# One term less in the softmax denominators of the second four heads, and one chunk's residual added by identity products

## The chip, the core and the metric

The kernel runs on one core of a Trainium2 chip. The metric is the device time of one execution in microseconds. Three runs of the kernel before gave 3167.57, 3167.66 and 3168.4 us; the median is 3167.66 us. All times below are of the kernel before.

## What is computed

The reference is one attention layer with a mask from an adjacency matrix, a feed forward part and three layer norms. There are F = 8 graphs of N = 2048 nodes with C = 256 channels, in H = 8 heads of D = 32 channels. Cut to what matters:

```
q, k, v = split(x @ w_qkv)                        # per head: N x 32
scores  = where(adj > 0, q k^T / sqrt(32), -1e9)
attn    = softmax(scores)                         # over the keys m
t       = attn @ v
y       = layernorm1(x + t)
z       = layernorm2(y + relu(y @ w1 + b1) @ w2 + b2)
out     = layernorm(x + z)                        # the last residual and norm
```

All of it is in 32-bit floats. The mask is added to the scores instead of being selected, and the softmax is not divided until the end: the exponentials are multiplied with v, their sums over the keys (the denominators) are found beside that, and the result is divided by them.

## The kernel before, in words

**Steps.** The main loop runs over `items` = (f, qc, g, mb): graph, chunk of 512 queries (4 of them), group of four heads (g = 0 or 1) and block of 128 keys (mb = 0 to 15). That makes 1024 steps of one block each; 16 steps are a group, 32 steps a chunk, 128 steps a graph. Step t issues, in this order: one piece of side work (`advance`), the exponentials of block t + 1 (L283, ScalarE), the scores of block t + 2 (L276, TensorE) with the mask added to them out of PSUM by VectorE (L279), and the products of block t with v (L310, TensorE). So TensorE's queue holds side work, scores, values, side work, and so on. A block is a tile `p` of 128 keys x 4 heads x 512 queries, 1 MB in 32-bit floats; 12 buffers hold such tiles.

**PSUM.** Six of the eight banks hold scores (three pairs; a block takes two pairs), one bank holds the sum of the value products, and one is left for side work. So at most one piece of side work can start in a step.

**Side work.** Generators in the list `fill` yield when they want to wait some steps, when they need the bank (BANK), when they could go on with the bank that they hold (MORE), or when they hold it and must wait (WAIT). The list is sorted by due time. `advance` gives each step a credit of 2200 units. One set of products (four of 128x512, one for each 32 columns of the array) costs 2048, four transposes cost 1400, so a step takes one such piece. A piece that is past its due time, or that stands in the way of one that is, goes on without credit, and then a step holds two sets. Side work is: turning x, projecting it to q, k and v for the next groups and the next graph, the denominators, the division (`outcome`, `divide`), and the `tail` of a chunk (norm, feed forward, norm, last residual, norm).

**Denominators.** The 16 blocks of a group are first added up to four tiles outside TensorE (`add_up`): the chain `POOLED` by GpSimd's `tensor_tensor` (L339), the two chains `MOVED` by accumulating DMAs that GpSimd issues (L336), and block 15 (`ALONE`) stays as it is. Then `denominator` multiplies the four tiles with `halves` (ones in 16 of 32 columns), one set of products a tile (L382), all into one PSUM bank. For g = 0 the sum is copied to `dT` (L385). For g = 1 it is added to `dT` by VectorE (L388), turned by TensorE (L95), and its reciprocal `rc` taken (L395); then `outcome` is started, which turns the two halves of the output, multiplies them with `rc` (L427) and adds the first residual by an accumulating DMA (L414).

The generator is started at step t + 2 after a group's last block t, with due time t + 8; the pooled tile is not used before step t + 3 and the second moved tile not before t + 4. The order on all queues is the order of issue, so a product whose tile is late holds up the scores and values behind it.

**The residual of the last graph's third chunk.** For (f, qc) = (7, 2) the first residual is no DMA: x is loaded early into the tile `xb` (L745, L746), and `outcome` has VectorE add it to y (L411, 128x1024, both operands in SBUF) before it starts the tail (which uses `xb` once more for its last residual). The very last group, `ENDING` = (7, 3, 1), has code of its own (`closing`) and is untouched.

Of the kernel before, what the change touches and what calls it, by code (L numbers as in the profile page):

```python
# [16 lines left out]
ALU = mybir.AluOpType  # L17
# [12 lines left out]
BANK, MORE, WAIT, TURNED, ROOM, INPUTS = -1, -2, -3, -4, -5, -10  # L30
# [31 lines left out]
def fast_path(ctx, tc, cst, x, adj, out, RS):  # L62
    nc = tc.nc
    F, N, C = x.shape
    NCK, TPC, MB = N // CH, CH // P, N // P
# [19 lines left out]
    ident, identb, wqkv, w1s, w2s = cst["ident"], cst["identb"], cst["wqkv"], cst["w1s"], cst["w2s"]  # L85
    state = {"pair": 0, "side": None, "turn": 0, "turned": False, "holder": None, "tails": 0, "credit": 0}

    def columns(out, lhsT, rhs, start, stop):
        state["credit"] -= 4 * out.shape[-1]
        in_columns(nc, out, lhsT, rhs, start, stop)  # L90
# [11 lines left out]
    def bank(dt=F32):  # L102
        shape = [P, CH] if dt == F32 else [P, 2, CH]
        if state["side"] is not None:
            i = 1 - state["side"]
            return ps_x[i].tile(shape, dt, name=f"x{i}")
        i = state["turn"]
        state["turn"] = (i + 1) % 5
        pool = ps_s[i] if i < 3 else ps_x[i - 3]
        return pool.tile(shape, dt, name=f"s{i}" if i < 3 else f"x{i - 3}")  # L110
# [140 lines left out]
    PT, O, OT, RC, DT = {}, {}, {}, {}, {}  # L251
# [63 lines left out]

    POOLED = (0, 3, 6, 8, 10, 12, 14)
    MOVED = ((1, 4, 7, 11), (2, 5, 9, 13))
    ALONE = 15  # L320

    SUM = 4

    def add_up(item):
        f, qc, g, mb = item
        if item[:3] == ENDING:
            h = mb // (MB // 2) * (MB // 2)
            if mb - h in (2, 4):
                first = PT[f, qc, g, h]
                nc.gpsimd.tensor_tensor(first, first, PT.pop(item), ALU.add)  # L330
            elif mb - h == 3:
                nc.gpsimd.dma_start(PT[f, qc, g, h + 1], PT.pop(item), accum_op=ALU.add)
            return
        for chain in MOVED:
            if mb in chain[1:]:
                nc.gpsimd.dma_start(PT[f, qc, g, chain[0]], PT.pop(item), accum_op=ALU.add)  # L336
        if mb in POOLED[1:]:
            first = PT[f, qc, g, POOLED[0]]
            nc.gpsimd.tensor_tensor(first, first, PT.pop(item), ALU.add)  # L339


# [24 lines left out]

    def denominator(f, qc, g, ready):
        grp = (f, qc, g)
        blocks = [ALONE, MOVED[0][0], POOLED[0], MOVED[1][0]]
        late = {2: ready - 1, 3: ready}  # L370
        yield BANK
        ps = bank()
        for n, block in enumerate(blocks):
            if n:
                yield MORE
            while state["now"] < late.get(n, 0):
                yield WAIT
            term = PT.pop((f, qc, g, block))
            state["credit"] -= 4 * CH
            for h in range(4):  # L380
                r = D * h
                nc.tensor.matmul(ps[r:r + D, :], cst["halves"][:, g, :], term[:, h, :], start=(n == 0), stop=(n == len(blocks) - 1))  # L382
        if g == 0:
            DT[f, qc] = op.tile([P, CH], F32, name="dT")
            nc.scalar.copy(DT[f, qc], ps)  # L385
            return
        dT = DT.pop((f, qc))
        nc.vector.tensor_tensor(dT, ps, dT, ALU.add)  # L388
        yield 1
        yield BANK  # L390
        ps = bank()
        transposes(ps, [dT[:, j::TPC] for j in range(TPC)])
        rc = RC[f, qc] = op.tile([P, TPC, H], F32, name="rc")
        den = ps.rearrange("p (j c) -> p j c", c=P)[:, :, ::D // 2]
        nc.vector.reciprocal(rc, den)  # L395
        nc.vector.tensor_tensor(RS[:, 0], RS[:, 0], den, ALU.add)
        nc.vector.tensor_tensor(RS[:, 1], RS[:, 1], den, ALU.min)
        begin = items.index((f, qc, g, LAST)) + SUM + 2
        start(begin, outcome(f, qc), begin)

    def outcome(f, qc):
        yield ROOM
        state["tails"] += 1
        xin = x[f, qc * CH:(qc + 1) * CH, :].rearrange("(p j) c -> p j c", p=P)
        y = yp.tile([P, TPC, C], F32, name="y")
        begin = items.index((f, qc, 1, LAST)) + SUM + 2
        yield from divide(f, qc, y)
        if (f, qc) == (F - 1, NCK - 2):
            yield 1
            xb = state["xb"]  # L410
            nc.vector.tensor_tensor(y, y, xb, ALU.add)  # L411
            start(begin + 3, tail(f, qc, y, xin, 2, xb), begin + 18)
            return
        nc.gpsimd.dma_start(y, xin, accum_op=ALU.add)  # L414
        if (f, qc) == (F - 1, NCK - 3):
            start(begin + 10, tail(f, qc, y, xin, 2), begin + 18)
        else:
            start(begin + 10, tail(f, qc, y, xin), begin + 26)
# [12 lines left out]
    def tail(f, qc, y, xin, per=1, xb=None):  # L431
        yield from norm(y, per)
        yield from feed_forward(y)
        if xb is not None:
            nc.gpsimd.tensor_tensor(xb, xb, rows(cst["be2r"]), ALU.add)
        yield 1
        z = y
        yield from norm(z, per if per == 1 else TPC)
        while xb is None and per > 1 and state["now"] % MB not in CALM:
            yield 1  # L440
        nc.gpsimd.tensor_tensor(z, z, rows(cst["g2r"]), ALU.mult)  # L441
        yield 1
        nc.gpsimd.tensor_tensor(z, z, rows(cst["be2r"]) if xb is None else xb, ALU.add)  # L443
        yield 1
        if xb is None:
            nc.gpsimd.dma_start(z, xin, accum_op=ALU.add)
            yield 7 if per == 1 else 10
        yield from norm(z, per)
        nc.sync.dma_start(out[f, qc * CH:(qc + 1) * CH, :].rearrange("(p j) c -> p j c", p=P), z)
        state["tails"] -= 1  # L450
# [155 lines left out]
    def start(t, gen, due):  # L606
        fill.append([t, gen, 1, due])
        fill.sort(key=lambda e: e[3])
# [120 lines left out]
    for t, (f, qc, g, mb) in enumerate(items):  # L729
        if g == 1 and mb % 2 and (f + 1 < F or qc + 1 < NCK):  # L730
            t0 = t
            while ((qc + 1) % NCK, mb // 2) not in MADE:
                advance(t0, finish=True)
                t0 += 1
            load_mask(f + (qc + 1) // NCK, (qc + 1) % NCK, mb // 2)
        while n_mask < MB and t >= 2 + 3 * n_mask:
            start(t, mask_job(n_mask), 3 * MB - 2 + 2 * n_mask if n_mask < MB // 2 else 4 * MB - 2 + 2 * n_mask)
            n_mask += 1
        for what, *which in (NEXT if f else {**NEXT, **LATER}).get(t % FRAME, []):
            to = f if what is ask and which[0] else f + 1  # L740
            if to < F:
                at = (0, 0, 0) if what is turn else (which[0], 0, 0) if what is ask else (0, which[1], which[0] * TPC)
                start(t, what(to, *which), t + 3 * MB if what is turn else items.index((to, *at)) - LEAD - 1)
        if t == len(items) - 2 * MB - 6:
            state["xb"] = take([P, TPC, C], F32)  # L745
            nc.sync.dma_start(state["xb"], x[f, qc * CH:(qc + 1) * CH, :].rearrange("(p j) c -> p j c", p=P))  # L746
        if t == len(items) - MB:
            xr, xb = state["rows"] = [take([P, TPC, C], F32) for _ in range(2)]
            nc.sync.dma_start(xr.rearrange("p (h j) c -> p h j c", h=2),
                              x[f, qc * CH:(qc + 1) * CH, :].rearrange("(h p j) c -> p h j c", h=2, p=P))  # L750
        if t == len(items) - MB + 6:
            nc.gpsimd.tensor_tensor(xb, xr, rows(cst["be2r"]), ALU.add)
        if t:
            advance(t)

        if t + 1 < len(items):
            exponentials(items[t + 1])
        if t + LEAD < len(items):
            nf, _, ng, nmb = items[t + LEAD]
            t0 = t  # L760
            while (nf, nmb // TPC, ng) not in V:
                advance(t0, finish=True)
                t0 += 1
            scores(items[t + LEAD])
        values(items[t])
        add_up(items[t])
        if mb == LAST and t + 1 < len(items):
            start(t + 2, denominator(f, qc, g, t + SUM), t + SUM + 4)
        for h in range(2):
            if t == len(items) - MB // 2 * (2 - h) + 4:  # L770
                start(t + 1, closing(h), len(items) - h)
    t = len(items)
# [244 lines left out]
```

## Time and profile before, and how to read it

| what | value |
|---|---|
| median of the runs | 3167.66 us |
| the profiled execution's own time | 3165.28 us |
| its span (first to last instruction) | 3163.5 us |
| granted TensorE clock | 0.995 of full speed |
| VectorE: mask added to the scores, L279, x2016 | 2371.1 us busy, 1218 ns each |
| ScalarE: exponentials, L283, x1024 | 1955.8 us busy, 1910 ns each |
| TensorE: scores L276 and values L310, x8064 each | 1152.4 and 1075.3 us busy |
| accumulating DMAs of tiles `p`, x380 | 1024.0 KB each, 10.1 us from issue to landing |

A row of the groups gives line, engine, operation, output <- inputs, count, then the busy time in us, the mean of one in ns, and the idle time of the engine ahead of it with what ended it. The profile shows a 32-bit product as two records, so a set of four products is 8 records; the four run side by side in the array. In the timeline the columns are start and duration in us, engine, line, operation, tiles, shape and count, and in brackets the idle time of the engine just before with what released it. The windows view gives busy time of PE (TensorE), PEld (weight loads), DVE (VectorE), ACT (ScalarE) and POOL (GpSimd) in a stretch of time.

### The profile page before, as it was taken

To read this page: it belongs to the slowest core of one execution; us is meant where nothing else is said; L and a number is where in the kernel's file an instruction comes from. 1 tells how busy PE (TensorE), PEld (TensorE's weight loads), DVE (VectorE), ACT (ScalarE), POOL (GpSimd) and SP (SyncE) were. 2 spreads that over 40 slices of the span, in tenths; PEclk is the share of its full clock that TensorE was granted. 3 is DMA by queue.
4 is the path that set the end of the run, shared out by engine and by line. 5 is a ranking of instruction groups with operands and counts; after the bars stand their busy time and mean duration, and the time that the engine had idled before them with its cause. 6 is when DMAs were issued, how large, how long until landed. Compare 5 with 4: busy or idle time off the path is not lost.

```text
span 3163.5 us, 68998 instructions
## 1 busy us (share of the span) xinstructions
PE 3071.6 (97%) x29220; PEld 969.5 (31%) x29220; DVE 2751.4 (87%) x3138; ACT 2423.8 (77%) x1934; POOL 2589.8 (82%) x1358
## 2 busy tenths in 40 slices
PE   8899999999999999999999999999999999999986
PEld 4222233222332233322333323323233323332223
DVE  4989888998888998888988898888888888889885
ACT  4777777777778877778877878777778777778774
POOL 1768888888888988888888888888889888889885
PEclk9999999999999999999999999999999999999998
DMA  8998888988888988789878888879879888888861
GB/s 255 224 213 187 189 184 182 205 189 192 178 176 202 198 186 182 167 197 218 186 168 187 191 199 192 180 174 204 193 172 205 178 192 193 177 174 167 174 149 42
DMA packets 165467, 586.89 MB, mean 186 GB/s; under 512 B 15360, under 2 KB 84480, under 8 KB 116512
## 3 DMA queue, kind: packets, MB, share of 16 engines
q0 software_dynamic: 63696, 430.60, 69.0%
q1 hardware_dynamic: 100640, 150.50, 14.1%
q8 instruction: 231, 3.78, 0.5%
q10 hardware_dynamic: 816, 1.31, 0.1%
q14 instruction: 84, 0.69, 0.1%
HBM read 146.15 MB, written 37.75 MB: 58 GB/s over the span
## 4 chain that ended last, share of the span: by engine, by line


## 5 line engine op out<-in xcount | busy, mean ns | idle before, releaser
L279 DVE TENSOR_TENSOR p<-s,mask 128x1024 f32<-128x1024 f32 x2016 | 2371.1, 1218 | 302.3 <-PE s L276 170.2
L283 ACT ACTIVATE p<-p 128x2048 f32<-128x2048 f32 x1024 | 1955.8, 1910 | 565.3 <-DVE p L279 458.2
L339 POOL TENSOR_TENSOR p<-p 128x2048 f32<-128x2048 f32 x378 | 1845.1, 4881 | 332.7 <-ACT p L283 332.2
L276 PE MATMUL s<-qT,kT 32*128 32x512 f32 x8064 | 1152.4, 640 | 48.1 <-DVE p L279 44.7
L310 PE MATMUL x<-p,v 128*32 128x512 f32 x8064 | 1075.3, 605 | 3.0 <-ACT oT L314 3.0
L276 PEld LDWEIGHTS s<-qT,kT 32*128 32x128 f32 x8064 | 315.5, 183 | 653.6 <-DVE p L279 627.7
L336 POOL DMA_DIRECT2D p<-p x378 | 406.5, 1076 | 69.7 <-ACT p L283 49.4
L310 PEld LDWEIGHTS x<-p,v 128*32 128x32 f32 x8064 | 158.7, 108 | 768.2 <-issue 303.5
L382 PE MATMUL x<-p,halves 128*32 128x512 f32 x2016 | 261.1, 592 | 0.3 <-ACT turned L575 0.3
L54 PE MATMUL x<-in,wqkv 128*32 128x512 f32 x1888 | 245.6, 592 | 1.5 <-DVE y L170 0.8
L360 ACT ACTIVATE y<-y,nb,rs 128x256 f32<-128x256 f32 x372 | 218.3, 591 | 1.5 <-POOL nb L357 1.4
L348 DVE BATCH_NORM_STATS2 st<-y 128x6 f32<-128x256 f32 x372 | 154.7, 416 | 0.0
L54 PE MATMUL x<-turned,w1s 128*32 128x512 f32 (+1 forms) x1024 | 127.1, 593 | 0.0
L54 PEld LDWEIGHTS x<-wqkv,in 128*32 128x32 f32 x3584 | 102.2, 110 | 62.9 <-issue 54.5
L54 PE MATMUL x<-w2s,hT 128*32 128x256 f32 x2016 | 120.3, 379 | 0.0
L54 PE MATMUL x<-wqkv,in 128*32 128x128 f32 x3584 | 117.1, 273 | 0.0
L382 PEld LDWEIGHTS x<-p,halves 128*32 128x32 f32 x2016 | 65.4, 110 | 149.8 <-issue 147.2
L54 PEld LDWEIGHTS x<-in,wqkv 128*32 128x32 f32 x1888 | 61.1, 110 | 143.4 <-issue 115.1
L354 POOL TENSOR_TENSOR rs<-rs,mhalf 128x4 f32<-128x4 f32 x93 | 96.2, 1035 | 7.7
L441 POOL TENSOR_TENSOR y<-y,g2r 128x1024 f32<-128x1024 f32 x31 | 100.4, 3240 | 0.0
L443 POOL TENSOR_TENSOR y<-y,be2r 128x1024 f32<-128x1024 f32 x30 | 92.1, 3071 | 0.6
L54 PEld LDWEIGHTS x<-w2s,hT 128*32 128x32 f32 x2016 | 65.4, 110 | 68.9 <-issue 35.3
(155 smaller groups left out, 1423.1 us busy)
## 6 DMA issues: line engine op xcount, KB each, us to landing
p<-p POOLq DMA_DIRECT2D x380, 1024.0 KB, 10.1
in<-xd SPq DMA_DIRECT2D x87, 512.0 KB, 8.7
mask<-md SPq DMA_DIRECT2D x248, 128.0 KB, 8.5
y<-in_x_dram POOLq DMA_DIRECT2D x60, 512.0 KB, 9.7
out_dram<-y SPq DMA_DIRECT2D x31, 512.0 KB, 5.9
in<-in_x_dram SPq DMA_DIRECT2D x30, 512.0 KB, 10.3
xd<-in SPq DMA_DIRECT2D x28, 512.0 KB, 8.3
p<-in_adj_dram SPq DMA_DIRECT2D x8, 1024.0 KB, 14.1
```

Source lines behind the costliest of these rows:

```text
L54: nc.tensor.matmul(out[r:r + D], lhsT[:, r:r + D], rhs, start=start, stop=stop)
L276: nc.tensor.matmul(ps2[half][:, j, :], KT[f, mb // TPC, g][r:r + D, (mb % TPC) * P:(mb % TPC + 1) * P], QT[f, qc, g][r:r + D, :], start=Tr ...
L279: nc.vector.tensor_tensor(pt[:, 2 * half:2 * half + 2, :], ps, MK[f, qc, mb // 2][:, mb % 2, None, :].to_broadcast([P, 2, CH]), ALU.add)
L283: nc.scalar.activation(PT[item], PT[item], AF.Exp, scale=1.0 / math.sqrt(D))
L310: nc.tensor.matmul(O[grp][r:r + D, :], V[f, mb // TPC, g][:, mb % TPC, r:r + D], PT[item][:, h, :], start=(mb == 0), stop=(mb == LAST))
L336: nc.gpsimd.dma_start(PT[f, qc, g, chain[0]], PT.pop(item), accum_op=ALU.add)
L339: nc.gpsimd.tensor_tensor(first, first, PT.pop(item), ALU.add)
L348: nc.vector.bn_stats(st, t[:, j, :])
L354: nc.gpsimd.tensor_tensor(rs, rs, cst["mhalf"], ALU.pow)
L360: nc.scalar.activation(t[:, j, :], t[:, j, :], AF.Identity, bias=nb[:, j:j + 1], scale=rs[:, j:j + 1])
L382: nc.tensor.matmul(ps[r:r + D, :], cst["halves"][:, g, :], term[:, h, :], start=(n == 0), stop=(n == len(blocks) - 1))
L441: nc.gpsimd.tensor_tensor(z, z, rows(cst["g2r"]), ALU.mult)
```

## The change

For g = 1 block 15 is no longer left alone: it becomes the last member of GpSimd's chain, which gets eight members instead of seven, and the moved chains shift by one block. `denominator` then has three tiles instead of four, is started two steps later, with late times and due time two steps later too. The group g = 0 stays as it is. Apart from this, in the third chunk of the last graph, the residual x is added to y not by VectorE from SBUF but with two sets of products of the identity with `xb`, whose results VectorE adds to y out of PSUM in two halves; the tail starts at the earliest one step later.

```diff
-    POOLED = (0, 3, 6, 8, 10, 12, 14)
-    MOVED = ((1, 4, 7, 11), (2, 5, 9, 13))
+    POOLED = ((0, 3, 6, 8, 10, 12, 14), (0, 3, 5, 7, 9, 11, 13, 15))
+    MOVED = (((1, 4, 7, 11), (2, 5, 9, 13)), ((1, 4, 8, 12), (2, 6, 10, 14)))
     ALONE = 15
...
-        for chain in MOVED:
+        for chain in MOVED[g]:
...
-        if mb in POOLED[1:]:
-            first = PT[f, qc, g, POOLED[0]]
+        if mb in POOLED[g][1:]:
+            first = PT[f, qc, g, POOLED[g][0]]
             nc.gpsimd.tensor_tensor(first, first, PT.pop(item), ALU.add)
...
     def denominator(f, qc, g, ready):
         grp = (f, qc, g)
-        blocks = [ALONE, MOVED[0][0], POOLED[0], MOVED[1][0]]
-        late = {2: ready - 1, 3: ready}
+        one, two = (chain[0] for chain in MOVED[g])
+        blocks = [one, POOLED[g][0], two] if g else [ALONE, one, POOLED[g][0], two]
+        late = {1 + (g == 0): ready - 1, 2 + (g == 0): ready}
...
         yield from divide(f, qc, y)
         if (f, qc) == (F - 1, NCK - 2):
-            yield 1
             xb = state["xb"]
-            nc.vector.tensor_tensor(y, y, xb, ALU.add)
-            start(begin + 3, tail(f, qc, y, xin, 2, xb), begin + 18)
+            for j in range(0, TPC, 2):
+                yield BANK
+                ps = bank()
+                columns(ps, ident, xb[:, j:j + 2, :].rearrange("p j c -> p (j c)"), start=True, stop=True)
+                nc.vector.tensor_tensor(y[:, j:j + 2, :], ps.rearrange("p (j c) -> p j c", c=C), y[:, j:j + 2, :], ALU.add)
+            start(begin + 4, tail(f, qc, y, xin, 2, xb), begin + 18)
             return
...
         if mb == LAST and t + 1 < len(items):
-            start(t + 2, denominator(f, qc, g, t + SUM), t + SUM + 4)
+            start(t + 2 + 2 * g, denominator(f, qc, g, t + SUM + 2 * g), t + SUM + 4 + 2 * g)
```

## The prediction

> **What bounds the kernel now.** The first part of the page comes first:
>
> ```profile
> PE 3071.6 (97%) x29220; PEld 969.5 (31%) x29220; DVE 2751.4 (87%) x3138; ACT 2423.8 (77%) x1934; POOL 2589.8 (82%) x1358
> ```
>
> TensorE (PE) looks like the bound, but VectorE and GpSimd are near it, and both get or lose work here. Next the groups that the change touches:
>
> ```profile
> L339 POOL TENSOR_TENSOR p<-p 128x2048 f32<-128x2048 f32 x378 | 1845.1, 4881 | 332.7 <-ACT p L283 332.2
> L336 POOL DMA_DIRECT2D p<-p x378 | 406.5, 1076 | 69.7 <-ACT p L283 49.4
> L382 PE MATMUL x<-p,halves 128*32 128x512 f32 x2016 | 261.1, 592 | 0.3 <-ACT turned L575 0.3
> ```
>
> L382 is 2016 records, 8 a set: 252 sets, 1.04 us busy each. PE waited 0.3 us ahead of them in all, so no sum of p came late. Then the timeline, cut at the first score product (L276) of each step. A step with one set of side work, and one without:
>
> ```profile
> 1728.49 1.14 PE L276 MATMUL s<-qT,kT 32*128 32x512 f32 x8
> 1729.56 1.06 PE L310 MATMUL x<-p,v 128*32 128x512 f32 x8
> 1730.44 1.04 PE L54 MATMUL x<-in,wqkv 128*32 128x512 f32 x8
> 1731.42 1.14 PE L276 MATMUL s<-qT,kT 32*128 32x512 f32 x8
> 1732.49 1.06 PE L310 MATMUL x<-p,v 128*32 128x512 f32 x8
> 1733.97 1.14 PE L276 MATMUL s<-qT,kT 32*128 32x512 f32 x8 [0.42 <-DVE p L279]
> ```
>
> From one L276 to the next is 2.93 us with a set, 2.55 without: the empty step is bound by VectorE, which masks two score tiles (2 x 1.218). So **an emptied slot is worth 2.93 - 2.55 = 0.38, not a set's 0.975** (2.925/3). A step made to take two sets is longer:
>
> ```profile
> 1659.70 1.14 PE L276 MATMUL s<-qT,kT 32*128 32x512 f32 x8
> 1661.66 1.93 PE L54 MATMUL x<-wqkv,in 128*32 128x128 f32 x64
> 1663.52 1.14 PE L276 MATMUL s<-qT,kT 32*128 32x512 f32 x8
> ```
>
> It takes 3.82, so **a double turned into two singles is worth 0.89**. VectorE's cover is read in the windows view, over the steps that hold a chunk's denominators and division:
>
> ```profile
> 1785.23:1808.34 23.11, 22.77 (x181) 6.90 (x177) 22.34 (x31) 15.48 (x9) 14.65 (x12) 1.00 0.63 138
> 1704.44:1708.22 3.78, 3.78 (x36) 0.99 (x32) 3.58 (x5) 1.96 (x2) 3.78 (x1) 1.00 1.03 210
> ```
>
> VectorE (third figure after the length) has 0.77 us free in the first 23.11 us, 0.59 of it in the first step, and 0.20 in the second stretch. What is taken from PE there is had only up to that.
>
> **What the Trainium skill says.** "GPSIMD Engine Reference", 3.1, has 4497 ns for a tensor_tensor add of 2048 32-bit elements; here adds in line start 4.5 us apart when nothing lies between. "SBUF — State Buffer", Who interferes with whom: a VectorE instruction with two SBUF inputs is fully blocked while a GpSimd instruction reads SBUF. The trace agrees:
>
> ```profile
> 3044.71 4.52 POOL L339 TENSOR_TENSOR p<-p 128x2048 f32<-128x2048 f32 x1 [0.28 <-ACT p L283]
> 3045.31 5.01 DVE L411 TENSOR_TENSOR y<-y,in 128x1024 f32<-128x1024 f32 x1
> 3051.51 2.09 PE L276 MATMUL s<-qT,kT 32*128 32x512 f32 x8 [5.06 <-DVE p L279]
> ```
>
> L411 ends 1.09 us after the add. "VectorE: DVE Perf Modes", The TRN2 errata, prices a 32-bit tensor_tensor at (N + 151)/0.96 ns: 1.22 us for 1024, so some 3.8 of the 5.01 is waiting.
>
> **The change, part by part.** There are 32 groups with g = 1; all but the last lose a set: 31. Write +k for k steps after a group's block 15.
>
> (1) Where the slot goes. In graphs 1 to 7 the four chunk ends differ.
> - After chunk 4 (7 times, at step 514 in the middle of the trace) the sets sit at +3 to +6. Now +3 is free. A projection to v waits there (its k was copied out at 1575, before; it ran at +10, +11), so it takes +3 and +4, the denominators +5 to +7, all that follows comes one slot earlier, and the double of 1659.70 becomes two singles. VectorE has 0.28 us free in that step and 1.26 in the next, so I count nearly all: 7 x 0.86 = 6.0.
> - After chunk 1 (7 times) w2 products fill the slots to +5; three sets follow at +6, +7 and, due, a double at +8 (1704.44). It becomes a single: 3.78 - 2.92 = 0.86, but VectorE has 0.20 there and 0.17 in the next step: 7 x 0.4 = 2.8 (bounds 0.2 and 0.86).
> - After chunk 2 (8 times) a turn of x whose load landed at 1775.4 can take +3; side work moves up and one more empty step comes, where VectorE may be full: 8 x 0.35 = 2.8 (0 to 0.4).
> - After chunk 3 (8 times, 1878.57) the next projection's loads landed at 1878.0 and 1880.8 and it waits five steps from issue, so +3 stays empty: 8 x 0.37 = 3.0. That slot ends before VectorE's full stretch, which then begins earlier.
> - The first graph's first chunk: 0.3. Sum **14.9 us**.
>
> (2) GpSimd. An add more for each of 31 groups: 31 x 4.881 = 151 us busy, 82% to 87%. It is hidden as long as the tiles are ready at +4, +5, +6. I laid out the tightest kind (chunk 3, before step +3 at 1878.57) with the trace's own ends of the exponentials and spacings: add 4.5, issue 0.65 to 0.8, g1 and be1 2.3 each, a norm's four small ones 2.2. The old chain idles around blocks 5 to 8 (2.2 and 1.3 us) and ends at 1880.8; the new one starts at block 5, has no such gap, and ends at 1881.7, against a use at 1886.0 (the old 1886.37 less 0.37). The first moved tile's last DMA is issued at 1870.4; with landings of 9 to 11 us it is there at 1879 to 1882, used at 1883.1. The second: issued 1875.6, there at 1885 to 1887, used at 1889.0. So 2 to 4 us stay. After chunk 2 the same comes out (1 to 3 us for the first tile); after 4 there is a step more, after 1 some 15 us. The longest landing in the trace is 14.3 us, so I take a wait of 0.1 us in each of the 16 tight groups, **1.5 us lost**. Bounds: nothing, and 2.5 us each. Moved DMAs stay six a group; their issue on GpSimd shifts by a block. SP's queue and its loads only follow the side work. Norms queue behind adds on GpSimd and ScalarE waits for them in order, with the exponentials behind; around 1859 the norm follows an add and ScalarE starts 0.06 us after it. In the new order it follows a DMA issue and is 1.4 us earlier; after chunk 2 it is 0.7 later, with 1.2 to spare. I take nothing (bounds -0.5 and +1 each). The 12 buffers: block 15 is released by an add ending near +4 instead of a product at +3, as many as before; nothing.
>
> (3) The residual. Gone: the stall of 5.06 us. Added: two sets in steps that were empty (2 x 0.38), two evictions of 128x512 like L427's 0.68 us beside them. The denominators there start two steps later but nothing else waits, and two more steps are empty. Steps from 3021.3 to 3068.0 took 46.7 us; laid out anew by kind (3 sets 2.93, 3 turns 2.74, 2 identity sets 2.93, 2 empty 2.58, 4 with norm statistics about 3.46) they take 41.9. The tail starts two steps later, so its last norm runs deeper in the end: -4.8 + 0.8 = **4.0 us saved** (bounds 1 and 6).
>
> Sum: 14.9 - 1.5 + 4.0 = 17.4 us. The profiled execution goes from 3165.28 to 3147.9 (span 3146.1); the median lies 2.38 above it, so 3167.66 - 17.4 = **3150.3 us**, its own range 3143 to 3156.
>
> **Rivals.**
> - Full price: PE is all that counts, each set is worth 0.975: 31 x 0.975 - 2 x 0.975 + 5.06 = 33: 3134. For: 97% busy. Against: the empty step at 1731.42.
> - Covered: empty slots give nothing as VectorE is full after them; only the doubles after chunk 4 and the residual count, 6 + 4 = 10: 3158. For: 0.77 us in 23 us. Against: 0.59 of it is in the very step that is emptied.
> - Late sums, some: a wait of 1 us in 16 groups eats 16: 3167, no change.
> - **Slower**: the first moved tile (last block 12, not 11) lands after +4, and scores behind it starve a VectorE that has no slack. The place is chunks 2 and 3; from 1.5 us a group (24 us) it decides against the 17.4 + 1.5. At 2.5 us: 40 - 18.9 = 21: 3189. For: GpSimd runs without a gap from block 5, landings up to 14.3. Against: the layout above.
>
> **Chances.** Forecast 0.60, full price 0.10, covered 0.15, some late 0.09, slower 0.06. Within 0.2% (6.3 us) is about what a measurement of this kernel can't tell from no change. Faster 0.85, same 0.09, slower 0.06. The range 3138 to 3167 takes in the covered and some-late cases and leaves out most of full price and slower, under 2 in 10.
>
> **What would show it.** L382 at 1768 records; L339 x409; empty steps of 2.55 at +3 after chunk 3; no 64-record step near block 9 of g = 1 after chunk 4; GpSimd near 2740 us; no 5 us L411. Wrong if L382 waits for POOL or a DMA by over 0.5 us a group, or if steps behind an empty one show PE waiting for DVE by as much as was saved.

## The result, and the profile after

The changed kernel takes 3158.14 us in the median of 8 runs (3156.47 to 3159.73), the kernel before 3167.91 us in 8 runs on the same chip. The ratio is 0.9969, with a 95% interval of 0.9960 to 0.9978: **9.8 us faster**, a little over half of the 17.4 us of the forecast. The time lies inside the wide range of the prediction (3138 to 3167), but above the range that its forecast gave itself (3143 to 3156). The profiled execution took 3158.02 us, its span 3155.97 us.

The first part of the page and the groups of the pooled sum and of the denominators, after:

```profile
PE 3051.3 (97%) x28988; PEld 962.6 (31%) x28988; DVE 2747.6 (87%) x3139; ACT 2427.1 (77%) x1934; POOL 2727.7 (86%) x1389
...
L339 POOL TENSOR_TENSOR p<-p 128x2048 f32<-128x2048 f32 x409 | 1999.9, 4890 | 221.3 <-ACT p L283 200.4
L383 PE MATMUL x<-p,halves 128*32 128x512 f32 x1768 | 231.1, 594 | 1.6 <-DVE kT L170 1.4
```

The denominators' sets (L383 now) have lost 248 records, 31 sets; GpSimd has 31 adds and 138 us more; and PE waited 1.6 us ahead of the sets in all, 1.4 of it for a tile of the mask jobs. So the sums are not late. VectorE's time is the same within 4 us. But PE waits for VectorE ahead of its scores more than before, 108 times in place of 90. These are the lines of PE's waits, first before, then after (us in all, times, the longest):

```profile
PE s L276 <- DVE p L279: 44.7, 90, 5.1
```

```profile
PE s L276 <- DVE p L279: 52.6, 108, 2.3
```

In the before figure is the one stall of 5.1 us at the old residual. Without it PE's waits for VectorE went from 40 to 53 us. That is a first sign of where a part of the missing gain went.

Cut at the first score product of a block, the two traces stand so (us; blocks are counted over the whole loop, so block 128 begins graph 1):

| stretch | before | after | difference |
|---|---|---|---|
| start and graph 0 | 436.34 | 439.27 | +2.9 |
| graph 1 to graph 7, chunk 3 | 2579.14 | 2569.59 | -9.6 |
| of these, one of graphs 2 to 6, mean | 381.37 | 379.94 | -1.4 |
| graph 7, chunk 4, up to the scores of block 1007 | 49.19 | 44.20 | -5.0 |
| the end, from there on | 98.84 | 102.91 | +4.1 |

The first row needs care. Over all twelve traces of this study graph 0 ends between 436.2 and 442.3 us, and the start alone lies between 53.2 and 57.5, with an order that is the same there. The profiled run of the kernel before was among the earliest. From the end of graph 0 on the traces repeat: graphs 2 to 6 take 379.93 to 379.95 us each after. The steady graphs give 7.2 of the 9.6 us and graph 7's first three chunks 2.8; graph 1 takes 0.4 us longer than before (382.58 against 382.19), and why it gains nothing was not worked out.

The forecast has 7.6 us more than the measured gain. Of these, 2.7 lie in the second row (12.3 forecast, 9.6 found) and 3.4 in the last two rows together (4.0 for the residual and 0.3 for the denominators forecast, 0.9 found). What is left, about 1.5, falls to the start and graph 0 when the medians are taken.

### The profile page after: what moved, and what is told of

It is laid out like the page before. It is cut to its first block, busy times and chain, and to the rows that moved or that the text cites. A ratio compares the mean times of both kernels' runs of the same rounds, so it can differ in the third digit from the quotient of the medians.

```text
span 3156.0 us, 68508 instructions
## 1 busy us (share of the span) xinstructions
PE 3051.3 (97%) x28988; PEld 962.6 (31%) x28988; DVE 2747.6 (87%) x3139; ACT 2427.1 (77%) x1934; POOL 2727.7 (86%) x1389
## 4 chain that ended last, share of the span: by engine, by line
## 5 line engine op out<-in xcount | busy, mean ns | idle before, releaser
L339 POOL TENSOR_TENSOR p<-p 128x2048 f32<-128x2048 f32 x409 | 1999.9, 4890 | 221.3 <-ACT p L283 200.4
L336 POOL DMA_DIRECT2D p<-p x378 | 416.2, 1104 | 49.2 <-ACT p L283 41.0
L383 PE MATMUL x<-p,halves 128*32 128x512 f32 x1768 | 231.1, 594 | 1.6 <-DVE kT L170 1.4
L360 ACT ACTIVATE y<-y,nb,rs 128x256 f32<-128x256 f32 x372 | 218.3, 591 | 0.5 <-POOL nb L357 0.5
L348 DVE BATCH_NORM_STATS2 st<-y 128x6 f32<-128x256 f32 x372 | 154.8, 416 | 0.0
L383 PEld LDWEIGHTS x<-p,halves 128*32 128x32 f32 x1768 | 57.3, 110 | 133.9 <-issue 126.5
```

The source lines that it names most:

```text
L348: nc.vector.bn_stats(st, t[:, j, :])
L360: nc.scalar.activation(t[:, j, :], t[:, j, :], AF.Identity, bias=nb[:, j:j + 1], scale=rs[:, j:j + 1])
```

## Experiments

| kernel | median, us | ratio to before, 95% |
|---|---|---|
| den_only | 3161.37 | 0.9977 (0.9966 to 0.9987) |
| res_only | 3167.76 | 0.9996 (0.9988 to 1.0004) |
| no_fifteen | 3158.31 | 0.9965 (0.9952 to 0.9979) |
| early | 3172.70 | 1.0013 (1.0007 to 1.0020) |
| first_old | 3157.79 | 0.9964 (0.9950 to 0.9978) |
| two_old | 3159.18 | 0.9967 (0.9955 to 0.9979) |
| gap | 3149.13 | 0.9934 (0.9921 to 0.9948) |
| three_stats | 3149.26 | 0.9934 (0.9920 to 0.9948) |
| before_gap | 3170.98 | 1.0005 (0.9998 to 1.0012) |
| gap_two_old | 3145.63 | 0.9926 (0.9913 to 0.9940) |

The kernel before had 3168.60, 3168.63 and 3168.87 us in the three comparisons.

**The two parts alone.** `den_only` is the changed kernel with the old residual; `res_only` is the kernel before with the new one.

```diff
-            for j in range(0, TPC, 2):
-                yield BANK
...
+            yield 1
+            nc.vector.tensor_tensor(y, y, xb, ALU.add)
+            start(begin + 3, tail(f, qc, y, xin, 2, xb), begin + 18)
```

> The changed kernel with the old residual of the last graph's third chunk (one VectorE add after the division); only the denominators and the sums are new. The forecast's own terms (1) and (2), 14.9 - 1.5 = 13.4 us saved, would give 3154.5. Theory from the two traces (a steady graph gains only 1.3 us, graph 0 loses 4.7 in one stall, graph 7's first three chunks gain 2.8, the start 1.1): 8 to 9 us saved, 3159 to 3160. If the 4.1 us that the end grew by come from the denominators (two more empty steps, sums ending later) and not from the residual, less than 6 saved, 3162 or more.

> The kernel before with only the residual as identity products. Forecast's term (3): 4.0 us saved, 3163.9. Theory: the stall of 5 us goes, but the tail of that chunk then runs about 4 us deeper into the end, so 0.5 to 1.5 us saved, 3166.4 to 3167.4; the end after step 1007 is longer than before by 3 to 4 us here too. Rival: the longer end belongs to the denominators; then the end is as before and 4 to 5 us are saved, 3163 to 3164.

The denominators alone save 7.2 us (3168.6 to 3161.4). That falls between the theory (8 to 9 us) and its rival (less than 6), so neither number came out. The residual alone saves 0.8 us, as its theory said; it can't be told from nothing. By the traces, graph 7's chunk 4 becomes 2.1 us shorter in den_only, 4.4 in res_only and 5.0 with both, and the end 2.0, 2.9 and 4.1 us longer. So the longer end belongs to both parts, more to the residual. What the residual's 4.4 us consist of is seen in the timelines, first of den_only, then of the changed kernel:

```profile
3040.45 4.85 POOL L339 TENSOR_TENSOR p<-p 128x2048 f32<-128x2048 f32 x1
3042.38 4.01 DVE L412 TENSOR_TENSOR y<-y,in 128x1024 f32<-128x1024 f32 x1
3047.58 1.48 PE L276 MATMUL s<-qT,kT 32*128 32x512 f32 x8 [4.05 <-DVE p L279]
```

```profile
3038.60 4.89 POOL L339 TENSOR_TENSOR p<-p 128x2048 f32<-128x2048 f32 x1
3038.71 1.04 PE L54 MATMUL x<-in,ident 128*32 128x512 f32 x8
3040.53 0.68 DVE L415 TENSOR_TENSOR y<-x,y 128x512 f32<-128x512 f32 x1
3041.64 1.04 PE L54 MATMUL x<-in,ident 128*32 128x512 f32 x8
```

The VectorE add with two inputs in SBUF takes 4.01 us and ends 1.1 us after the GpSimd add beside it; an add of half the size with one input in PSUM, under a GpSimd add of the same length, takes 0.68 us. In "SBUF — State Buffer", Who interferes with whom, the Trainium skill says that a VectorE instruction with at most one SBUF input, outside the modes that use two ports, does not contend with GpSimd; the 0.68 us agree.

Why the end is longer is seen around the last copy of the output oT, first before, then after. L490 (L494 after) are the denominators' products of the last group's closing halves, L467 (L471 after) the norms of the two halves, L360 the last norm of chunk 3's tail.

```profile
3123.46 1.91 PE L490 MATMUL x<-p,halves 128*32 128x256 f32 x32
3123.71 0.37 ACT L303 COPY oT<-x 128x256 f32<-128x256 f32 x1 [2.38 <-PE x L298]
3134.09 1.09 ACT L467 ACTIVATE y<-y,nb,rs 128x256 f32<-128x256 f32 x2 [10.01 <-DVE nb L465]
...
3150.56 2.31 ACT L467 ACTIVATE y<-y,nb,rs 128x256 f32<-128x256 f32 x4 [3.25 <-DVE nb L465]
...
3158.23 1.09 ACT L467 ACTIVATE y<-y,nb,rs 128x256 f32<-128x256 f32 x2 [0.19 <-DVE nb L465]
```

```profile
3113.18 4.50 PE L494 MATMUL s<-p,halves 128*32 128x256 f32 x80
3113.43 0.37 ACT L303 COPY oT<-x 128x256 f32<-128x256 f32 x1 [1.19 <-PE x L298]
3125.50 1.09 ACT L471 ACTIVATE y<-y,nb,rs 128x256 f32<-128x256 f32 x2 [11.69 <-DVE nb L469]
...
3142.36 1.09 ACT L471 ACTIVATE y<-y,nb,rs 128x256 f32<-128x256 f32 x2 [5.21 <-DVE nb L469]
3143.35 1.08 ACT L360 ACTIVATE y<-y,nb,rs 128x256 f32<-128x256 f32 x2
...
3150.03 1.09 ACT L471 ACTIVATE y<-y,nb,rs 128x256 f32<-128x256 f32 x2 [0.19 <-DVE nb L469]
```

The tail's last norm (L360) now stands between the norms of the halves, and one might blame it. But from 3150.56 to 3158.23 before, and from 3142.36 to 3150.03 after, it is 7.67 us both times, so that costs nothing. The time is lost ahead of it. The later tail holds up the closing halves' sums, which start right behind its last w2 products: 18.9 us ahead of the last copy of oT before, 15.4 after. So 80 records of them (4.50 us) are left at the copy, against 32 (1.91 us), and the first norm of the halves starts 12.1 us after the copy, against 10.4. That is 1.7 of the 4.1 us. Of the others 1.3 lie ahead of the copy, and 1.1 in small pieces behind. den_only and res_only also have 80 records left there, and from the last copy to the end they take 41.5 and 42.4 us, the changed kernel 42.5, the kernel before 39.8. So each part alone makes the tail late enough. This is read from the traces; no run moves the tail alone.

**GpSimd's added adds.** `no_fifteen` leaves block 15 of the second four heads out of the sums: the added work is gone, and the three sets stay.

```diff
-    POOLED = ((0, 3, 6, 8, 10, 12, 14), (0, 3, 5, 7, 9, 11, 13, 15))
-    MOVED = (((1, 4, 7, 11), (2, 5, 9, 13)), ((1, 4, 8, 12), (2, 6, 10, 14)))
+    POOLED = ((0, 3, 6, 8, 10, 12, 14), (0, 3, 6, 8, 10, 12, 14))
+    MOVED = (((1, 4, 7, 11), (2, 5, 9, 13)), ((1, 4, 7, 11), (2, 5, 9, 13)))
```

> The changed kernel with block 15 of the second four heads left out of the sum altogether (the old sums without the fourth set; this leaves out part of the denominators), so that three sets remain and GpSimd's added 31 adds are gone: 151 us less on GpSimd. Theory: those adds are hidden, the time is that of the changed kernel within 1.5 us: 3156.6 to 3159.6. Rival: GpSimd's work costs 3 us or more, by late sums or by VectorE and ScalarE waiting for it (the norms), and it comes to 3155 or less; at the forecast's 1.5 us, 3156.6.

The first part of its page:

```profile
PE 3053.1 (97%) x28988; PEld 963.4 (31%) x28988; DVE 2748.5 (87%) x3139; ACT 2427.7 (77%) x1934; POOL 2587.6 (82%) x1358
```

GpSimd has 140 us less to do, and the time is the same, 3158.31 against 3158.14. The added adds are hidden, as far as these runs can tell. The order of the sums leaves another trace: in all eight kernels with the new chains the moved tiles' DMAs landed after 9.0 to 9.3 us (median), in all four with the old chains, this one among them, after 10.0 to 10.1.

**How much slack the sums have.** `early` takes the delay of two steps away.

```diff
-            start(t + 2 + 2 * g, denominator(f, qc, g, t + SUM + 2 * g), t + SUM + 4 + 2 * g)
+            start(t + 2, denominator(f, qc, g, t + SUM), t + SUM + 4)
```

> The changed kernel without its two steps of delay: the three sets may start two steps after block 15, and the sums are asked for 5.4 to 5.9 us earlier. The forecast's layout said that 2 to 4 us of slack are left at +4 to +6 after chunks 2 and 3: then PE waits 2 to 4 us for a sum in 16 groups or more, 32 to 64 us: 3190 to 3222, and the denominators' sets show waits for POOL or DMA. Rival: the delay isn't needed, side work ahead of the sets holds them back anyway: 3155 to 3162.

Both were wrong: it costs about 14 us. The group of the sets in its page, and the place after chunk 3 in its timeline:

```profile
L383 PE MATMUL x<-p,halves 128*32 128x512 f32 x1768 | 230.5, 593 | 14.5 <-DMA p<-p 12.2
```

```profile
1889.01 1.07 PE L310 MATMUL x<-p,v 128*32 128x512 f32 x8
1891.05 1.06 PE L383 MATMUL x<-p,halves 128*32 128x512 f32 x8 [0.98 <-DMA p<-p]
```

After chunk 3 the first set can now run at +3, and there it waits 0.98 us for the first moved tile; the step takes 4.11 us. In the changed kernel that set runs at +5, two steps of 2.94 us later, so some 4.9 us of slack are left; at +4, where the forecast put it, it would be 2.0. The chunk windows of graph 4 that hold the other ends differ from the changed kernel by 0.00, 0.00 and 0.53 us: after chunks 4 and 1 the last w2 products fill the slots up to +3, so the sets can't run earlier anyway. After chunk 2 they run at +3 without a wait for a sum, but PE then waits for VectorE in the turns. So in graph 4 a sum is late after one chunk end of four.

**Graph 0.** In the changed kernel's graph 0 stands a stall of 5.01 us that the kernel before has in milder form (1.83 us). ScalarE and those behind it, after:

```profile
164.33 0.62 ACT L161 CAST turned<-turned 128x512 bf16<-128x512 int32 x1 [5.01 <-DMA turned<-in_adj_dram]
166.82 1.94 PE L310 MATMUL x<-p,v 128*32 128x512 f32 x8 [3.11 <-ACT p L283]
```

A cast of the mask job stands in ScalarE's queue ahead of the exponentials and waits for its load. `first_old` gives graph 0 the old denominators; `two_old` gives them to graph 0 and to graph 7's chunk 3.

```diff
+    def new(f, qc, g):
+        return int(g == 1 and f > 0)
...
-        for chain in MOVED[g]:
+        n = new(f, qc, g)
+        for chain in MOVED[n]:
...
-            start(t + 2 + 2 * g, denominator(f, qc, g, t + SUM + 2 * g), t + SUM + 4 + 2 * g)
+            late = 2 * new(f, qc, g)
+            start(t + 2 + late, denominator(f, qc, g, t + SUM + late), t + SUM + 4 + late)
```

In two_old the condition has `and (f, qc) != (F - 1, NCK - 2)` added.

> The changed kernel, but graph 0 keeps the old denominators (four sets) and sums; 28 groups are left with three sets. Theory: the stall of 5 us in graph 0 (ScalarE waiting for an adjacency load at 164 us) is made by the order, so it goes: 4.7 us won less 4 slots at 0.3, so 3154.5 to 3155.5. Rival: the stall is the time at which a load happens to land, whatever the order; then nothing is won and the 4 slots are lost: 3159 to 3160, and a wait of 4 us or more stays in graph 0.

> The changed kernel, but graph 0 and the last pooled group (graph 7, chunk 3) keep the old denominators; 27 groups have three sets. Theory: graph 0's stall is gone (by the trace of first_old, chunk 2 of graph 0 takes 96.99 us in place of 101.86, less 0.6 for the lost slots), and the last chunk with the end is 0.6 shorter (-4.39 + 2.86 = -1.5 with the residual alone, -0.9 with both): 3153 to 3154. Rival: the run of first_old (3157.8) tells the truth and the trace of graph 0 doesn't: 3157 or more.

The medians (3157.79 and 3159.18) give neither theory its gain; first_old lies between its two numbers, two_old where its rival put it. The twelve traces say more. The wait ahead of this cast is 4.95 to 5.35 us in the five kernels with the new sums in graph 0, and 1.8 to 1.9 us in the seven with the old ones. So the order makes the stall, and the rival of first_old, that it depends on when a load happens to land, is out. Chunk 2 of graph 0 takes 101.7 to 102.0 us in the four kernels with the full new order there, 97.0 to 98.9 in the others. Counted from the first score product to the end of graph 0, these four take 385.6 to 386.1 us, mean 385.9; the six with the old order there 381.9 to 385.8, mean 383.3. So the order costs about 2.6 us in graph 0 by the traces, not 4.7. The start, ahead of the first score product, moves by 4.3 us from trace to trace, more than this, and the medians of first_old and two_old don't confirm it.

**VectorE beside the turns.** Here a loss was found that one line gives back. The timelines of PE and VectorE after chunk 4 in the middle of the trace, first before. L348 is a quarter of the statistics of the tail's second norm (0.42 us, with its aggregate 0.60), L388 (L389 after) the addition of dT, L95 the turns.

```profile
1594.52 1.04 PE L382 MATMUL x<-p,halves 128*32 128x512 f32 x8
1596.12 0.42 DVE L348 BATCH_NORM_STATS2 st<-y 128x6 f32<-128x256 f32 x1
...
1603.30 1.04 PE L382 MATMUL x<-p,halves 128*32 128x512 f32 x8
1604.88 0.68 DVE L388 TENSOR_TENSOR dT<-x,dT 128x512 f32<-128x512 f32 x1
1605.48 0.42 DVE L348 BATCH_NORM_STATS2 st<-y 128x6 f32<-128x256 f32 x1
1606.34 0.74 PE L95 MATMUL x<-ident,dT 128*128 128x128 f32 x4
1607.29 1.14 PE L276 MATMUL s<-qT,kT 32*128 32x512 f32 x8 [0.21 <-DVE p L279]
```

```profile
1603.82 1.04 PE L383 MATMUL x<-p,halves 128*32 128x512 f32 x8
1605.40 0.68 DVE L389 TENSOR_TENSOR dT<-x,dT 128x512 f32<-128x512 f32 x1
1606.00 0.42 DVE L348 BATCH_NORM_STATS2 st<-y 128x6 f32<-128x256 f32 x1
1606.86 0.74 PE L95 MATMUL x<-ident,dT 128*128 128x128 f32 x4
1607.84 1.14 PE L276 MATMUL s<-qT,kT 32*128 32x512 f32 x8 [0.24 <-DVE p L279]
1608.83 0.42 DVE L348 BATCH_NORM_STATS2 st<-y 128x6 f32<-128x256 f32 x1
1609.99 0.72 PE L95 MATMUL x<-ident,oT 128*128 128x128 f32 x4
1611.04 1.14 PE L276 MATMUL s<-qT,kT 32*128 32x512 f32 x8 [0.33 <-DVE p L279]
```

The statistics begin behind the first set and come one a step. A step with a set lasts 2.92 us and has VectorE's 2.34 us of masks in it, so it takes up 0.58 us of other work. Behind the last set the addition of dT joins the quarter, and that step, the one with the turn of dT, takes 3.02 us before and 3.05 after. Four sets bring four quarters to that point; three bring three. The fourth (1608.83) then falls into the step with the first turn of oT, which VectorE's own work fills: that step takes 3.19 us in place of 2.75. PE waits 0.24 us ahead of it, as it did before (0.21), and 0.33 us behind it, which is new. Two experiments test it. `gap` leaves one step to other side work between dT's addition and its turn (first diff). `three_stats` keeps the order on TensorE and leaves out the statistics of the fourth quarter, which is scaled by the third's (second diff).

```diff
         nc.vector.tensor_tensor(dT, ps, dT, ALU.add)
-        yield 1
+        yield 1 if f == 0 or (f, qc) == (F - 1, NCK - 2) else 2
```

```diff
         for j in range(TPC):
-            st = small.tile([P, nc.vector.BN_STATS_DIM], F32, name="st")
...
+            if j < n:
+                st = small.tile([P, nc.vector.BN_STATS_DIM], F32, name="st")
...
-        yield from norm(z, per if per == 1 else TPC)
+        yield from norm(z, per if per == 1 else TPC, TPC - 1 if per == 1 else TPC)
```

> The changed kernel with one line more: between the addition of the denominators (dT) and the turn of dT one step is left to other side work (not in graph 0 and not in the last chunk before the ending). Theory: three sets no longer cover the four steps in which the tail before has its norm statistics (0.60 us of VectorE a step), so one of them falls on the turns of dT and oT, and PE waits there 0.63 us a chunk (0.24 + 0.34 + 0.05 after chunks 4 and 1, 0.24 + 0.14 after chunk 2); a step with a projection in between gives VectorE the time: 5 to 9 us faster than the changed kernel, 3149 to 3153. Rival: VectorE is full over the whole stretch and its debt only moves to the next empty steps: within 2 us of the changed kernel, 3156 to 3160.

> The changed kernel with the same order on TensorE, but the second norm of every tail (not of the last two chunks) leaves out the statistics of its fourth quarter and scales that quarter by the third's (this leaves out part of the norm): 0.60 us of VectorE less in the step in which the turns of dT begin, 30 times, 18 us in all. If VectorE's load in these steps is what took the freed slots' worth, PE's waits of 0.63 and 0.38 us a chunk go, 22 chunks or so, and the empty steps behind lose their debt: 8 to 13 us faster than the changed kernel, 3145 to 3150. Rival: the gain of the gap came from its other order of side work (doubles undone, loads met) and not from VectorE: within 2 us of the changed kernel, 3156 to 3160.

Both theories' numbers for VectorE came out: 9.0 and 8.9 us faster than the changed kernel, whose interval of 0.9960 to 0.9978 lies clear of both. The same place in gap, then in three_stats:

```profile
1601.63 0.68 DVE L389 TENSOR_TENSOR dT<-x,dT 128x512 f32<-128x512 f32 x1
1602.22 0.42 DVE L348 BATCH_NORM_STATS2 st<-y 128x6 f32<-128x256 f32 x1
1602.97 1.06 PE L54 MATMUL x<-wqkv,in 128*32 128x128 f32 x32
1605.06 0.41 DVE L348 BATCH_NORM_STATS2 st<-y 128x6 f32<-128x256 f32 x1
...
1609.07 0.75 PE L95 MATMUL x<-ident,dT 128*128 128x128 f32 x4
1609.75 1.14 PE L276 MATMUL s<-qT,kT 32*128 32x512 f32 x8
1611.82 0.75 PE L95 MATMUL x<-ident,oT 128*128 128x128 f32 x4
1612.49 1.14 PE L276 MATMUL s<-qT,kT 32*128 32x512 f32 x8
```

```profile
1605.56 1.14 PE L276 MATMUL s<-qT,kT 32*128 32x512 f32 x8 [0.23 <-DVE p L279]
1607.62 0.75 PE L95 MATMUL x<-ident,oT 128*128 128x128 f32 x4
1608.30 1.14 PE L276 MATMUL s<-qT,kT 32*128 32x512 f32 x8
```

In gap a projection to v stands where the turn of dT stood, and at this place the waits in the turns are gone (after chunk 1 one of 0.32 us stays, and after chunk 3 new ones come). In three_stats the wait of 0.33 us is gone, and the one of 0.24, ahead of the missing quarter, stays. In graph 4 the steps with turns of dT and oT take 35.01 us after, 33.05 in gap and 33.60 in three_stats.

`before_gap` puts the same line into the kernel before.

> The kernel before with only the free step ahead of the turn of dT. If the crowd on VectorE is made by the change (three sets in place of four beside four norm statistics), the kernel before has little to win by it: its steps of dT and oT take 34.26 us a graph against 33.05 with the gap, 1.2 a graph, 7 graphs: 3159 to 3162 if nothing is given back, 3162 to 3166 if half is. Rival: the gap is a gain of its own, as large before as after (9 us): 3159 or less. Then the changed denominators are worth 10 us with the gap as without; under the first theory they are worth 14 or more with it, 3163 against 3149.

It gains nothing (3170.98 against 3168.87), which is less than even its theory said (3159 to 3166). In graph 4 the steps of dT and oT do get shorter (34.26 to 32.96 us), but other steps give most of it back. From graph 1 to graph 7's chunk 3 the line takes 1.2 us off the kernel before and 10.1 off the changed one. So the crowd is for the most part the change's own. With the line on both sides the new denominators and residual are worth 21.8 us by the medians in place of 9.8, and 18.5 in place of 9.6 in that stretch of the traces. The kernel before without the fourth quarter was not run, so three_stats alone doesn't tell how much a lighter VectorE would win there too.

**Both edits.** `gap_two_old` is gap with the old denominators in graph 0 and in graph 7's chunk 3.

> Both edits together: the step left free ahead of the turn of dT, and the old denominators in graph 0 and in graph 7's chunk 3. If both theories hold they add up, for they lie in different graphs: 3158 - 4.5 - 7 = 3146.5, between 3144 and 3149. If neither holds, 3157 to 3160.

At 3145.63 us it is the fastest here, 23.0 us under the kernel before, and where the two theories together put it. But its interval overlaps that of gap, so only the line of gap is shown to matter.

## Why the forecast was right in direction and too large

**What held.** Three sets for four, 31 times; the doubles near block 9 undone (graph 4 has no step of 64 records, and its denominators have no double any more); GpSimd hidden; the two residual sets in steps of 2.93 us; VectorE as the limit of an empty step. GpSimd came to 2727.7 us, near the 2740 of the prediction.

**Step (1), the slots: mis-sized, in part by the cover of VectorE's work.** From graph 1 to graph 7's chunk 3 the forecast comes to 12.3 us (14.9 - 1.5, less 0.8 for graph 0 and 0.3 for the last chunk); the traces show 9.6. In a steady graph two doubles went and two empty steps came, as forecast: 2 x 0.88 + 2 x 0.37 = 2.5 us at full worth. Of that, in graph 4, the turns took back 0.75 (34.26 to 35.01) and the four empty steps 0.26 by being 2.616 us long and not 2.551, so 1.5 was left. "VectorE has 0.28 us free in that step and 1.26 in the next, so I count nearly all" failed: the free time lay in the step of the old double, while the work that lost its cover, the fourth quarter of the statistics, lay ahead of it. The windows view in the prediction, with VectorE free for 0.77 us in 23.11, gave a warning of this, but only after chunk 1 was the gain cut by half for it. The places were partly wrong too. After chunk 4 the projection to v did not take +3; the w2 products moved there, and the denominators went directly behind them at +4 to +6. After chunk 3 it was the other way round: +3 did not stay empty, since projections to v took +3 and +4 (1879.77 and 1882.71), and the denominators came at +5 to +7. The number of empty steps was still right.

**Step (2), late sums: too much.** 1.5 us was set aside, 0.2 us was measured as wait for a DMA, and no_fifteen shows no cost. The layout's 2 to 4 us of slack were not far off: after chunk 3 early shows 2.0 us at +4. The sets came a step later than laid out, at +5, and so had 4.9.

**Step (3), the residual: the body right, the end wrong.** The body shrank by 5.0 us (4.8 forecast). The end grew by 4.1, against 0.8. The tail's start, later by a step or two, was priced as a last norm that runs deeper into the end. That norm costs nothing where it stands now. What the price left out is that the later tail holds up the sums of the closing halves on TensorE. The net of the last chunk is 0.9 us, not 4.0.

**The rivals.** Covered (3158) gave the nearest number, and VectorE's load, its cause, is what gap and three_stats point to. That the number fits so well is luck: from graph 1 to graph 7's chunk 3 the slots gave 9.6 us where it counted 6, and the last chunk 0.9 where it counted 4. Full price, late sums and slower fell.

What stays open is why graph 1 gained nothing, and why the runs of first_old and two_old don't show the 2.6 us of graph 0.

## What to carry to other kernels

A slot that is taken off a busy engine is also a step of cover for another engine. Before pricing it, list what the second engine does in that step and in the next ones, quarter by quarter, and ask where that work goes. When one line of spacing wins as much as the change did, it may only undo a crowd that the change made, so test it on the old kernel as well. Work moved towards the end of a kernel is priced by what it holds up there, not by its own length.

## What the runs showed of the hardware

A step with one set of four products of 128x512, its scores and its values took 2.92 to 2.93 us in at least 97% of such steps between graph 1 and graph 7's chunk 3, in every trace. Graphs 2 to 6 of the changed kernel agree within 0.02 us, yet the end of graph 0 lay between 436.2 and 442.3 us over the traces. Accumulating DMAs of 1024 KB landed after 9.0 to 9.3 us (median) in the eight kernels with the new chains and after 10.0 to 10.1 in the four with the old ones, though as many are issued. And 140 us of GpSimd adds, running beside VectorE's masks with one input in PSUM, cost no time that could be measured.
